# Scatters of an attention mask, issued by the state of a pacing clock instead of one per scan unit

## The chip, the cores and the metric

The kernel runs on one core of a Trainium2 chip. The metric is the device time of one execution in microseconds (us). The engines are called as in the profile: PE is TensorE, DVE is VectorE, ACT is ScalarE, POOL is GpSimd, SP is SyncE, which here only issues transfers.

## The reference

The input is four images of 32 x 32 positions with 256 channels, so 1024 tokens per image. Four layers follow each other:

- layer 0: layer norm, a projection to 512 channels, a 3 x 3 depthwise convolution, and a state space scan over the 1024 tokens with 64 states per channel, then a projection back and a residual;
- layer 1: a bottleneck with a grouped 3 x 3 convolution;
- layer 2: attention with 8 heads under a mask, then a mixture of 8 experts;
- layer 3: another state space scan with 16 states per channel, and a second mixture of experts.

The change concerns the mask of layer 2. It is built once from a list of edges and used for all four images:

```python
mask = jnp.zeros((N, N), dtype=bool).at[edge_index[0], edge_index[1]].set(True)
scores = jnp.where(mask[None, None], scores, -jnp.inf)
```

The scans are recurrences, for each channel d and state n:

```python
h = dA * h + (dtt * xt)[:, :, None] * Bt[:, None, :]
y = jnp.einsum('bdn,bn->bd', h, Ct)
```

## The kernel before, in words

**The scans.** The generator `scans` runs the recurrences as 1280 units in a fixed order of (layer, image), `SCANS`: image 0 of layer 0 first, units 0 to 255, four groups of 128 channels with 64 units each. A unit is 128 rows of 1024 steps. It loads `dA` with SP, takes its exponential on ACT, spreads the input over the rows with a matmul (`ps_rep`, two PSUM buffers), multiplies it by B on VectorE (`ps_rep<-ps_rep,rows`), runs the recurrence on VectorE (the SCAN instruction, `h<-dA,ps_rep`), and multiplies h by C on GpSimd (`h<-h,rows`, five buffers for h). Every two units TensorE collects h into `ps_y`, two units late. `scans` yields twice per unit.

**The side work.** Everything else is cut into `STAGES`, generators that yield after small pieces: four `front` stages (layer 0 up to its scan), `middle` (the rest of layer 0, layers 1 and 2, and layer 3 up to its scan) and `last`, one for each image. The first `front` also runs the preparation of weights (`prepare`). At its end each front makes the scan's inputs in eight items of 512 tokens (`steps`): ACT computes `sp_e` and `sp_l`, VectorE one operation on `sp_e`, GpSimd three on `sp_l` and `sp_r`, ACT and VectorE split the result into three bfloat16 `parts` (`sp_x` is the rest between them), GpSimd makes the last part, SP stores them. A stage that needs a scan's result waits (`Wait`) until that scan is issued: `middle` of image 0 needs all four groups of scan (0,0).

**The order.** Nothing is scheduled by hand on a time axis. The program wraps the engines in `Metered`, which adds an assumed cost of each instruction to a clock of its engine; `run` issues half a unit of a scan, and then pieces of side work until some clock is ahead of VectorE's. Every clock is held to at most 4 us (`LAG`) behind VectorE's. The assumed costs are the kernel's own: for GpSimd 2.3 ns a column for `tensor_tensor`, and 1.0 us for an indirect DMA.

**The mask.** The generator `mask_work` (`setup`, then `mask_prepare`, then `scatter`) sorts the edges' positions and then issues one indirect DMA after another on GpSimd, each of which writes 128 zeros into a DRAM tile that was filled with a large negative number (`mask_dram<-zero,where`). 64 are always issued. For 480 more there are four tests on GpSimd (`value_load` and `Switch`, lines 1134 and 1136) that jump over 32, 64, 128 and 256 of them when no row of edges has that many entries; with these inputs they are all jumped over. Then one DMA copies the mask to bfloat16 (`maskT<-mask_dram`, line 1142). The tile is read first by SP at line 1215, in the attention of image 0. `mask_work` is advanced in two places: in `need`, once for every piece of a stage that a scan has to wait for (this issues 22 scatters before unit 0), and in `run`, at every second yield of `scans`, that is behind each unit:

```python
for n, _ in enumerate(self.scans(mp, psum)):
    if n % 2:
        next(self.mask_work, None)
    now = clock["vector"]
```

So in the kernel before, the 42 scatters that are left stand one behind each of the units 0 to 41, the four tests behind units 43 to 46, and the copy behind the next.

Of the kernel before, what the change touches and what calls it, by code (L numbers as in the profile page):

```python
# [132 lines left out]
class Hybrid:  # L133
# [428 lines left out]
    def run(self):  # L562

        self.done, self.ready = set(), set()
        self.todo, self.stage, self.wait = list(STAGES), None, None
        self.alone = False
        nc, tc = self.nc, self.tc
        with tc.tile_pool(name="scan", bufs=1) as mp, tc.tile_pool(
            name="scps", bufs=1, space=PSUM
        ) as psum, tc.tile_pool(name="sdps", bufs=1, space=PSUM) as side, tc.manual_schedule():  # L570
            self.side_psum(side)
            self.mask_work, self.sorted = self.setup(), False
            clock = self.clock = dict.fromkeys(Metered.COST, 0.0)
            self.nc = Metered(nc, clock)
            for n, _ in enumerate(self.scans(mp, psum)):
                if n % 2:
                    next(self.mask_work, None)
                now = clock["vector"]
                for e in clock:
                    clock[e] = max(clock[e], now - LAG)  # L580
                for _ in range(TICKS):
                    if max(clock.values()) > clock["vector"] + LEAD or self.advance() is None:
                        break
            while self.advance() is not None:
                pass
            self.nc = nc
        assert not self.todo
# [588 lines left out]
    def attention(self, b, tb):  # L1176
        nc, tc, vec = self.nc, self.tc, self.vec
        with tc.tile_pool(name=f"at{b}", bufs=1, side="right") as op:
            xa = op.tile([P, TB, C], F32, name="xa")
            qT = op.tile([P, 2, L], F32, name="qT")  # L1180
            kT = op.tile([P, 2, L], F32, name="kT")
            v = op.tile([P, TB, C], F32, name="v")
            mT = op.tile([P, 2, L], BF16, name="mT")
            maskT = op.tile([P, TB, L], BF16, name="maskT")
            wo = self.weight(op, "L2_attn_Wo", 2)
            large = op.tile([1, 1], I32, name="large")
            nc.vector.memset(mT, 0.0)
            with tc.tile_pool(name=f"aa{b}", bufs=1, side="right") as fp:
                wq, wk, wv = (self.weight(fp, "L2_attn_" + n, 2) for n in ("Wq", "Wk", "Wv"))
                xT = fp.tile([P, 2, L], F32, name="xTa")  # L1190
                yield from self.norm(fp, tb, TB, xa, "lnt")
                yield from self.turned(xa, TB, xT)

                def project(item):
                    w, dst, bias, sc, c, g = item
                    ps = self.ps("ps_qk")
                    cols = slice(g * 512, (g + 1) * 512)
                    self.mm(ps, lambda k: w[:, k, c * P : (c + 1) * P], xT, 2, cols)
                    nc.scalar.activation(
                        dst[:, c, cols], ps, AF.Identity, bias=bias[:, c : c + 1], scale=sc  # L1200
                    )

                yield from self.pipe(
                    [
                        (w, dst, bias, sc, c, g)
                        for w, dst, bias, sc in (
                            (wq, qT, self.bq, self.isq), (wk, kT, vec["L2_attn_bk"], 1.0)
                        )
                        for c in range(2) for g in range(2)
                    ],  # L1210
                    project, cost=1.7,
                )

                yield from self.large_scores(fp, qT, kT, large)
                nc.sync.dma_start(maskT, self.mem[("maskT",)].rearrange("j p f -> p j f"))

                def values(j):
                    ps = self.ps("ps_v", (P, 2, C))
                    for i in range(2):
                        m = 2 * j + i  # L1220
                        for k in range(2):
                            nc.tensor.matmul(
                                ps[:, i, :], lhsT=xT[:, k, m * P : (m + 1) * P], rhs=wv[:, k, :],
                                start=(k == 0), stop=(k == 1),
                            )
                    nc.scalar.copy(v[:, 2 * j : 2 * j + 2, :], ps)

                yield from self.pipe(range(TB // 2), values, cost=1.7)
            go = nc.values_load(large, engines=self.sides, min_val=0, max_val=1)
            tc.mark_branch_hint_location(f"large{b}", go, engines=self.sides)  # L1230
            yield from self.add_rows(xa, self.bo, TB)
            yield from self.add_rows(tb, self.beta, TB)
            with tc.tile_pool(name=f"ab{b}", bufs=1, side="right") as fp:
                yield from self.shift(fp, qT, kT, mT, maskT, go, f"large{b}")
            with tc.tile_pool(name=f"ac{b}", bufs=1, side="right") as fp:
                yield from self.all_heads(fp, tb, qT, kT, v, maskT, mT, xa, wo)
# [694 lines left out]
```

## Time and profile before

| what | us |
|---|---|
| time, median of 3 runs (lowest to highest) | 6504.83 (6499.96 to 6507.34) |
| profiled execution, its own time | 6499.29 |
| its span in the profile | 6497.3 |
| VectorE busy | 5119.6 |
| TensorE busy | 5253.9 |
| GpSimd busy | 3646.8 |
| unit 0 of the scans starts (VectorE's timeline) | 152.6 |
| unit 258 starts | 1247.4 |

The span goes from the first to the last profiled instruction; the time of the execution is 2.0 us longer. A row of a timeline or of the groups reads: start and duration, engine, line, operation, written tile, read tiles, shapes, and in brackets the idle time of the engine before it with what ended it. A row of the table of stretches reads: the stretch, its length, busy time of each engine with its number of instructions, TensorE's granted clock, the share of the DMA engines' time, and GB/s. Nearly all instructions carry line 124, the helper that meters them, so they are told apart by tile.

### The profile page before, as it was taken

The page shows a single profiled execution, that of the slowest core. Times are in us where ns is not written, and L with a number is a line of the kernel's source. Part 1 is how long each engine was busy: PE and PEld are TensorE (multiplying, and loading weights), DVE is VectorE, ACT ScalarE, POOL GpSimd, SP SyncE. Part 2 cuts the span into 40 slices and gives each one's busy share as a digit, 9 for nine tenths or more (in the row PEclk, how much of TensorE's full clock was granted, in tenths as well). Part 3 has the DMA queues.
Part 4 walks back from the last instruction along what each step waited for, and adds up shares of the span by engine and source line. Part 5 has one row for each costly group of instructions (what it writes and reads, how often), then busy time and mean ns, then how long its engine had stood idle before and what let it go on. Part 6 is the DMA issues. An engine that isn't in the chain of part 4 may idle for free. (4 is left out here: it accounts for less than half of the span.)

```text
span 6497.3 us, 59722 instructions
## 1 busy us (share of the span) xinstructions
PE 5253.9 (81%) x20235; PEld 2124.1 (33%) x20320; DVE 5119.6 (79%) x4310; ACT 3415.4 (53%) x4095; POOL 3646.8 (56%) x1793
## 2 busy tenths in 40 slices
PE   6667868689797569979689679798699688978979
PEld 2022212222342022234145232252255222524656
DVE  3978988988898998889889988898899981258311
ACT  3346656355576335567568445577387354246311
POOL 2957677765557666555856665556756661055200
PEclk9577868689898569979789789898699689878989
DMA  2454554643355566335635664345544750156221
GB/s 101 145 163 159 180 163 160 198 150 124 119 174 170 180 169 164 113 128 184 195 132 176 195 159 135 112 146 178 182 164 163 196 148 15 46 147 166 68 67 34
DMA packets 348077, 936.58 MB, mean 144 GB/s; under 512 B 37140, under 2 KB 119648, under 8 KB 346144
## 3 DMA queue, kind: packets, MB, share of 16 engines
q1 hardware_dynamic: 345616, 930.35, 46.0%
q0 software_dynamic: 2128, 2.13, 0.2%
q8 instruction: 168, 2.75, 0.2%
q14 instruction: 165, 1.35, 0.1%
HBM read 842.59 MB, written 93.95 MB: 144 GB/s over the span
## 5 line engine op out<-in xcount | busy, mean ns | idle before, releaser
L124 POOL TENSOR_TENSOR h<-h,rows 128x1024 f32<-128x1024 f32 x1280 | 3033.0, 2372 | 1835.8 <-DVE h L124 1572.9
L124 DVE TENSOR_TENSOR_SCAN h<-dA,ps_rep 128x1024 f32<-128x1024 f32 x1280 | 2923.7, 2284 | 131.4 <-ACT dA L124 3.1
L124 DVE TENSOR_TENSOR ps_rep<-ps_rep,rows 128x1024 f32<-128x1024 f32 x1280 | 1551.7, 1212 | 188.5 <-PE ps_rep L124 183.9
L124 ACT ACTIVATE dA<-dA,A_L_conv_A_log 128x1024 f32<-128x1024 f32 x1024 | 1147.7, 1144 | 612.1 <-DMA dA<-dt 547.2
L124 PE MATMUL ps_rep<-S,spread_L_conv_A_log 96*128 96x512 bf16 x2048 | 763.2, 463 | 767.6 <-DVE h L124 716.2
L124 PE MATMUL ps_y<-h,collect_L_conv_A_log 128*32 128x512 f32 x4096 | 775.8, 767 | 61.5 <-POOL h L124 61.0
L124 PE MATMUL ps_h<-xTm,we 128*128 128x512 f32 x1536 | 714.2, 604 | 0.0
L124 PE MATMUL ps_e<-we,h_m 128*128 128x256 f32 x3072 | 700.4, 380 | 2.3 <-ACT h_m L124 2.3
L124 PEld LDWEIGHTS <-spread_L_conv_A_log 96*128 96x128 bf16 x2048 | 159.9, 103 | 1568.9 <-DVE h L124 1236.1
L124 ACT ACT_TABLE_LOAD x483 | 619.7, 1283 | 59.4 <-PE ps_h L124 44.1
L124 PEld LDWEIGHTS ps_e<-we,h_m 128*128 128x128 f32 x3072 | 579.4, 190 | 152.5 <-issue 61.1
L124 DVE SCALAR_TENSOR_TENSOR tb<-ps_e,cw,tb 128x256 f32<-128x256 f32 x512 | 219.9, 474 | 409.3 <-PE ps_e L124 409.2
L124 ACT ACTIVATE h_m<-ps_h,cols 128x512 f32<-128x512 f32 x384 | 260.2, 687 | 501.4 <-PE ps_h L124 498.9
L124 ACT ACTIVATE p<-ps_sc 128x512 f32<-128x512 f32 x432 | 234.5, 594 | 386.0 <-PE ps_sc L124 255.4
L124 PEld LDWEIGHTS ps_h<-xTm,we 128*128 128x128 f32 x1536 | 291.9, 193 | 331.7 <-issue 286.9
L124 ACT ACTIVATE dA<-dA,A_L_attn_A_log 128x1024 f32<-128x1024 f32 x256 | 290.6, 1146 | 200.0 <-DMA dA<-dt 172.3
L124 PE MATMUL ps_rep<-S,spread_L_attn_A_log 96*128 96x512 bf16 x512 | 185.8, 451 | 173.8 <-DVE h L124 161.0
L124 PE MATMUL ps_at<-p,v 128*32 128x512 f32 x1024 | 277.6, 623 | 4.8 <-ACT sums L124 4.6
L124 PE MATMUL ps_at<-p,ones 128*32 128x512 f32 x1024 | 277.6, 623 | 0.0
L124 PE MATMUL ps_sc<-qT,kT 32*128 32x512 f32 x864 | 262.9, 665 | 14.2 <-ACTq L1318 8.1
L124 PE MATMUL ps_cv<-pad,diag 128*128 128x512 f32 x576 | 262.3, 597 | 0.0
L124 PEld LDWEIGHTS ps_y<-h,collect_L_conv_A_log 128*32 128x32 f32 x4096 | 99.4, 119 | 436.9 <-issue 222.6
(327 smaller groups left out, 4865.4 us busy)
## 6 DMA issues: line engine op xcount, KB each, us to landing
dA<-dt SPq DMA_DIRECT2D x1280, 512.0 KB
we<-in_L_ffn_W_dram SPq DMA_DIRECT2D x64, 512.0 KB
parts<-parts SPq DMA_DIRECT2D x64, 384.0 KB
S<-parts SPq DMA_DIRECT2D x96, 256.0 KB
dt<-sp_r SPq DMA_DIRECT2D x64, 256.0 KB
y<-yo SPq DMA_DIRECT2D x128, 128.0 KB
y_back<-y SPq DMA_DIRECT2D x64, 256.0 KB
we<-in_L_ffn_w_dram SPq DMA_DIRECT2D x64, 256.0 KB
```

Of the source, the lines that this page charges most:

```text
L124: return got(*args, **kw)
```

## The change

There are two edits. In `run`, the mask's generator is advanced behind a unit only if GpSimd's pacing clock is behind VectorE's at that point; `now` is read one line earlier for that. In `attention`, whatever is left of the generator is issued before the mask is loaded.

```diff
@@ -573,9 +573,9 @@
             clock = self.clock = dict.fromkeys(Metered.COST, 0.0)
             self.nc = Metered(nc, clock)
             for n, _ in enumerate(self.scans(mp, psum)):
-                if n % 2:
+                now = clock["vector"]
+                if n % 2 and clock["gpsimd"] < now:
                     next(self.mask_work, None)
-                now = clock["vector"]
                 for e in clock:
                     clock[e] = max(clock[e], now - LAG)
                 for _ in range(TICKS):
@@ -1212,6 +1212,8 @@
                 )
 
                 yield from self.large_scores(fp, qT, kT, large)
+                for _ in self.mask_work:
+                    pass
                 nc.sync.dma_start(maskT, self.mem[("maskT",)].rearrange("j p f -> p j f"))
 
                 def values(j):
```

In the order of the built instructions this moves the scatters: those behind units 0 to 2 stay, the next 39 stand behind units 20 to 58, the four tests behind units 60 to 63, and the copy behind the next. Since a scatter also adds 1.0 us to GpSimd's pacing clock, the side work of the fronts is let through at other units too.

## The prediction

> **What bounds the kernel now.** I read, in this order, the busy shares of the page, the table of stretches, the waits and the timeline of GpSimd, and the timelines of VectorE and TensorE where VectorE stood still.
>
> ```profile
> span 6497.3 us, 59722 instructions
> PE 5253.9 (81%) x20235; PEld 2124.1 (33%) x20320; DVE 5119.6 (79%) x4310; ACT 3415.4 (53%) x4095; POOL 3646.8 (56%) x1793
> ```
>
> VectorE's 79% is an average: up to about 5300 us, where the scans run, it stands near 90%, and then a TensorE tail follows. I count scan units from 0 (the n-th SCAN row of VectorE's timeline). A unit with no side work takes 3.54 us (units 70 to 90 start 3.54 apart): a 1.21 us multiply and a 2.29 us scan. Every microsecond that VectorE loses in a unit is lost for good. These stretches are units 0 to 43, 43 to 55, 55 to 60, 60 to 93, 93 to 98, and five late items of front 3 (units 228 to 242):
>
> ```profile
> core 0: us, PE busy (x) PEld busy (x) DVE busy (x) ACT busy (x) POOL busy (x), PEclk, DMA share, GB/s
> 152.60:317.00 164.40, 111.97 (x255) 14.68 (x254) 151.47 (x91) 71.43 (x75) 150.23 (x92) 0.58 0.43 145
> 317.00:383.30 66.30, 35.62 (x77) 4.95 (x76) 48.46 (x31) 25.75 (x33) 47.87 (x29) 0.55 0.62 181
> 383.30:432.40 49.10, 23.77 (x62) 8.56 (x60) 30.32 (x58) 10.17 (x12) 18.20 (x10) 0.60 0.53 163
> 432.40:550.80 118.40, 114.36 (x388) 43.62 (x389) 112.83 (x67) 82.62 (x113) 76.69 (x33) 0.97 0.46 158
> 550.80:581.70 30.90, 23.20 (x71) 6.71 (x69) 19.05 (x13) 19.27 (x26) 16.77 (x9) 0.89 0.41 130
> 1121.60:1183.10 61.50, 42.29 (x100) 5.58 (x96) 60.88 (x41) 38.31 (x49) 60.72 (x36) 0.53 0.58 188
> ```
>
> In the first row, where the scatters are, GpSimd is as full as VectorE; in the fourth, where front 1 convolves, GpSimd is 65% busy. GpSimd's timeline shows why:
>
> ```profile
> 320.06 1.00 POOL L124 DMA_INDIRECT mask_dram<-zero,where  x1 [0.17 <-issue]
> 321.09 2.36 POOL L124 TENSOR_TENSOR h<-h,rows 128x1024 f32<-128x1024 f32 x1
> 330.26 2.35 POOL L124 TENSOR_TENSOR h<-h,rows 128x1024 f32<-128x1024 f32 x1 [6.82 <-issue]
> 336.98 1.15 POOL L124 TENSOR_TENSOR parts<-sp_x,parts 128x512 bf16<-128x512 f32 x1 [4.36 <-DVE ps_rep L124]
> 346.52 2.35 POOL L124 TENSOR_TENSOR h<-h,rows 128x1024 f32<-128x1024 f32 x1 [2.19 <-issue]
> ```
>
> A unit with a scatter costs GpSimd 2.37 + 0.17 + 1.00 = 3.54 us, VectorE's own pace, so nothing it does for front 0 (1.15 + 3 x 1.26 = 4.9 us an item) can be made up. The idle times of 6.82, 4.36, 2.19 and once more 4.36 us (before the multiply at 353.23) are the four tests on whether more scatters are needed, 17.7 us together. When GpSimd is late, TensorE's ps_y stands in front of the next ps_rep, and VectorE stops:
>
> ```profile
> 275.56 1.93 PE L124 MATMUL ps_y<-h,collect_L_conv_A_log 128*32 128x512 f32 x6 [7.50 <-POOL h L124]
> 278.50 1.23 DVE L124 TENSOR_TENSOR ps_rep<-ps_rep,rows 128x1024 f32<-128x1024 f32 x1 [5.02 <-PE ps_rep L124]
> 335.60 1.23 DVE L124 TENSOR_TENSOR ps_rep<-ps_rep,rows 128x1024 f32<-128x1024 f32 x1 [4.74 <-PE ps_rep L124]
> 342.71 2.16 DVE L124 TENSOR_TENSOR sp_x<-sp_l,parts 128x512 f32<-128x512 f32 x1 [5.88 <-ACT parts L124]
> ```
>
> [...] a scatter occupies 1.00 us, its landing takes 3.0 us (median of the 42 beside scans). [...]
>
> **The change part by part.** *Order.* The order of the built instructions, before against after, shows the counts and kinds unchanged. [...] All the side work of fronts 0 to 3 that followed unit 4 stands closer: from the preparation (units 55 to 60, now 21 to 26) on it is exactly 34 units earlier, with its own pattern kept. It ends near unit 220; then 38 bare units wait for scan (0,0). From unit 260 on the order is as before. Why: the pacing clock charged GpSimd 2.42 + 1.00 a unit against VectorE's 3.55, a credit of 0.13; without the scatter it is 1.13, and an item of front 0 is let through every third unit. The drain before the mask load costs nothing: the list is empty 224 units earlier. SP's 2,055 transfers move with their stages; none is added.
>
> *Sum, as excess over 3.54 us a unit.* Before: units 0 to 43, 164.4 - 152.2 = 12.2; 43 to 55, 66.3 - 42.5 = 23.8; 55 to 60, 49.1 - 17.7 = 31.4; 60 to 93, 118.4 - 116.8 = 1.6; 93 to 98, 30.9 - 17.7 = 13.2; 98 to 258, no different in the two kernels.
>
> After:
> - *Front 0's six items, units 0 to 21.* Same spacing as in the last row of the table: (61.5 - 15 x 3.54) / 5 = 1.7 us an item, 10 for six; 3 more since the first two stand two units apart. 13 in place of 36.0: **23 gained**. VectorE's own work for the items stays; the stalls go. Next late there is ACT's parts, 2 to 6 us late where items crowd (11.7 us in units 43 to 55); the 3 allows for one.
> - *Preparation, units 21 to 26.* 31.4 again. A unit lasts 9.8 us there, which covers a 3.5 us GpSimd turn; the mask copy (2 MB, landing 13.7 us) no longer precedes it, which could gain some microseconds, and a scatter caught in its loads could lose as many. Taken at 0, bounds -5 to +5.
> - *Scatters beside front 1, units 26 to 59.* GpSimd's turn of 3.54 to 3.55 us against 3.54 loses up to 0.01 x 34 = 0.3. What else stands behind a waiting scatter is the next h multiply, then ps_y. A scatter waits for its predecessor's landing; in units 0 to 43 that was 4.7 us in six waits, at a DMA share of 0.43, here 0.46. GpSimd can be about two units (7 us) late before TensorE notices, as few front operations need it there. **1 lost**, bounds 0 to 6; if the cover goes it is the 5.
> - *The tests, units 60 to 63.* The first two (11.2 us) fall in stalls that front 1 has there anyhow (VectorE waits 5.5 us for ps_rep, then 3.8 for sp_e). The last two and the late multiplies push front 1's first sp_l: recorded to end at 577.8, it would end near 559.1 + 6.8 + 2.4 + 4.4 + 2.4 + 2.2 + 2.4 + 4.4 + 3.8 = 587.9. VectorE's sp_x behind it comes 10 us later, and the items that follow keep GpSimd 98% busy, so nothing is won back. **10 lost**, bounds 0 [...] to 17.7. Before, the tests cost inside the 23.8.
> - *Bare units 220 to 258*: 3.54 us each, nothing to lose.
>
> Together 23 - 1 - 10 = **12 us gained**. After unit 260 the same instructions follow in the same order, so the gain is carried through VectorE's stretch to the tail. The profiled execution took 6499.3 us (span 6497.3), 5.5 under the median of 6504.8; its own sum is 6487.3, and at the median 6492.8, which I give as 6493.
>
> **The rivals.** *The tests are hidden whole* by front 1's stalls or run during the multiplies: 23 gained, 6482. For it: 9.3 us of stalls stand there; against it: 17.7 us do not fit, and in units 43 to 50 the tests did stop VectorE. *The loss is only moved*: the tests cost all 17.7 and scatters 5 in their new place, 23 - 23 = 0, 6505. For it: the same turns and tests meet a front that is dense on VectorE and ScalarE. *Scatters land late beside front 1*, and that ends slower. Each has 2.37 + 0.17 us of multiply to hide its landing in. If the mean wait for landing were 1.3 us, GpSimd's turn would be 4.85, and 39 scatters less 7 us of lateness allowed would lose 44: 23 - 10 - 44 = 31 slower, 6536. It decides from a mean wait of about 0.5 us ((12 + 1 + 7) / 39). Against it: the wait before was 4.7 / 42 = 0.11. For it: landings beside scans reached 5.7 us. *The change does nothing* can be ruled out, since the order of instructions differs.
>
> **How the numbers follow.** A measurement of this kernel can tell about 0.2%, 13 us. Main case 0.6, half of it over 13; hidden tests 0.17, all over; loss moved 0.14, nearly all within; late scatters 0.09, mostly slower. Faster 0.47, same 0.44, slower 0.09. The range goes from hidden tests with a lighter preparation, 6475, to the loss moved plus 5 us of preparation, 6510. The main case's own range is 6485 to 6502.
>
> **What would show it.** In the profile after: unit 21 starts near 152.6 + 21 x 3.54 + 13 = 240 (before 231), unit 55 near 152.6 + 55 x 3.54 + 13 + 31 + 3 = 394 (before 383.3), unit 64 near 152.6 + 64 x 3.54 + 13 + 31.4 + 2.6 + 23.2 = 449, unit 258 near 1235 (before 1247.4). GpSimd's waits for mask_dram beside front 1 under 8 us would confirm the scatter term; VectorE's idle time at units 60 to 66 is the tests' term. Units 0 to 21 with more than 25 us of excess, or a time that returns after unit 258, would make me wrong.

## The result, and the profile after

The changed kernel takes 6487.2 us (median of 18 runs, 6478.1 to 6496.4) against 6504.6 us (18 runs, 6493.0 to 6515.2): a ratio of 0.9973, 95% interval 0.9965 to 0.9980, that is 17 us less, between 13 and 23. The forecast was 12 less.

The head of the page of the changed kernel:

```profile
span 6481.8 us, 59799 instructions
PE 5240.9 (81%) x20320; PEld 2121.8 (33%) x20320; DVE 5121.5 (79%) x4310; ACT 3415.5 (53%) x4095; POOL 3649.2 (56%) x1793
```

Busy times are as before (TensorE's 5241 us against 5254, the others within 3 us); what changed is idle time. The table of stretches of the changed kernel, cut at its units 0, 21, 26, 59 and 64, and from 64 to 220 and 220 to 258:

```profile
core 0: us, PE busy (x) PEld busy (x) DVE busy (x) ACT busy (x) POOL busy (x), PEclk, DMA share, GB/s
156.50:241.90 85.40, 54.52 (x130) 7.82 (x132) 84.06 (x55) 57.17 (x71) 81.57 (x48) 0.52 0.55 173
241.90:290.80 48.90, 24.56 (x62) 9.71 (x60) 30.29 (x59) 10.38 (x13) 21.98 (x14) 0.53 0.52 161
290.80:413.90 123.10, 117.19 (x388) 44.26 (x389) 112.90 (x66) 82.34 (x113) 106.96 (x63) 0.96 0.49 158
413.90:458.00 44.10, 25.76 (x71) 6.88 (x69) 20.64 (x13) 19.34 (x26) 21.41 (x13) 0.72 0.38 116
458.00:1102.50 644.50, 468.49 (x1426) 127.47 (x1426) 596.29 (x403) 395.98 (x514) 496.70 (x257) 0.71 0.56 178
1102.50:1237.50 135.00, 74.75 (x228) 8.84 (x228) 129.60 (x77) 43.82 (x41) 89.53 (x39) 0.50 0.52 164
```

In the first row VectorE is busy 84.1 of 85.4 us while front 0 finishes. In the third GpSimd is now 107 us busy of 123, against 77 of 118 in the same work before: the scatters have moved here. The fourth, with the tests, lasts 44.1 us against 30.9 of the same front work before. The fifth is the same work as the kernel before did in this row of its own table:

```profile
581.70:1233.20 651.50, 472.26 (x1426) 128.44 (x1426) 596.72 (x404) 396.21 (x514) 497.14 (x257) 0.71 0.54 177
```

As excess over 3.54 us a unit, which is how the prediction counts:

| work | before | forecast | after |
|---|---|---|---|
| front 0's rest (after: units 0 to 21; before: 0 to 55, with scatters and tests) | 36.0 | 13 | 11.1 |
| preparation (21 to 26; before 55 to 60) | 31.4 | 31.4 | 31.2 |
| front 1's convolution (26 to 59; before 60 to 93) | 1.5 | 2.6 | 6.3 |
| start of front 1's items (59 to 64; before 93 to 98) | 13.2 | 23.2 | 26.4 |
| the rest of the fronts (64 to 220; before 98 to 254) | 99.3 | 99.3 | 92.2 |
| bare units (220 to 258; before 254 to 258) | 0.0 | 0 | 0.5 |
| sum (of the unrounded values) | 181.5 | 169.5 | 167.7 |

So units 0 to 258 took 1081.0 us instead of 1094.8. Unit 0 started 3.9 us later in this execution, and units 258 to 1279 took 4804.3 us instead of 4810.7. Both are differences between executions: over the twelve profiles, runs of both kernels and of all variants below that load 12 units ahead, the start lies anywhere from 151.4 to 156.8 us, the later stretch from 4800 to 4814, and neither goes with the order of instructions.

GpSimd's timeline of the changed kernel where the tests stand, and VectorE behind it:

```profile
420.50 1.00 POOL L124 DMA_INDIRECT mask_dram<-zero,where  x1 [3.03 <-DMA mask_dram<-zero,where]
428.22 2.38 POOL L124 TENSOR_TENSOR h<-h,rows 128x1024 f32<-128x1024 f32 x1 [4.33 <-issue]
436.07 2.35 POOL L124 TENSOR_TENSOR h<-h,rows 128x1024 f32<-128x1024 f32 x1 [5.47 <-issue]
442.89 2.34 POOL L124 TENSOR_TENSOR h<-h,rows 128x1024 f32<-128x1024 f32 x1 [4.48 <-PE ps_dt L124]
449.47 1.26 POOL L124 TENSOR_TENSOR sp_l<-sp_l,sp_e 128x512 f32<-128x512 f32 x1 [4.24 <-issue]
454.10 2.16 DVE L124 TENSOR_TENSOR sp_x<-sp_l,parts 128x512 f32<-128x512 f32 x1 [13.65 <-ACT parts L124]
```

The rows are a late scatter, then three multiplies and front 1's first sp_l, each behind one of the four tests. (By GpSimd's own multiplies the tests stand behind units 59 to 62, and behind 42 to 45 in the kernel before, one unit earlier than counted above.) VectorE's sp_x stands in front of all that VectorE has to do next, and waits 13.65 us. So GpSimd's late turn is still there, in one place.

### The profile page after: what moved, and what is told of

Its sections match the earlier page's. It is cut to its first block, busy times and chain, and to the rows that moved or that the text cites. A ratio compares the mean times of both kernels' runs of the same rounds, so it can differ in the third digit from the quotient of the medians.

```text
span 6481.8 us, 59799 instructions
## 1 busy us (share of the span) xinstructions
PE 5240.9 (81%) x20320; PEld 2121.8 (33%) x20320; DVE 5121.5 (79%) x4310; ACT 3415.5 (53%) x4095; POOL 3649.2 (56%) x1793
## 5 line engine op out<-in xcount | busy, mean ns | idle before, releaser
L124 PE MATMUL ps_y<-h,collect_L_conv_A_log 128*32 128x512 f32 x4096 | 744.1, 767 | 15.6 <-POOL h L124 15.6
L124 POOL TENSOR_TENSOR sp_l<-sp_l,sp_e 128x512 f32<-128x512 f32 x62 | 78.5, 1266 | 276.5 <-DVE sp_e L124 252.3
```

The lines of the kernel that those rows point to most:

```text
L124: return got(*args, **kw)
```

## The experiments

The theory: GpSimd was full where the scatters stood (busy 150 of 164 us in units 0 to 43), and the tests made it later (17.7 us of idle time); in the new place both cost less but not nothing. All ratios are against runs of the kernel before on the same chip.

**Both kernels once more.** No edit.

> The changed kernel once more, unaltered. Theory (a full GpSimd and the four tests explain the gain, all of it before unit 64): 0.9973 of before again; units 0 to 64 last within 1 us of the first profile of the changed kernel (156.5 to 458.0), while the 7 us that units 64 to 220 and the 6 us that units 258 to 1279 took less than in the profile of before are differences between executions and come out otherwise. Rival (the earlier side work also speeds up what follows): both come out again within 2 us.

> The kernel before once more, unaltered, for a second profile. Both theories: within 0.2% of before. Theory: units 0 to 64 take what they took (152.6 to 448.0, within 1 us or so), units 98 to 254 may differ from the 651.5 us of the first profile by as much as the changed kernel's 644.5 did.

The changed kernel came to 0.9970 of before (0.9960 to 0.9980), the kernel before to 0.9997 (0.9988 to 1.0005). Of the changed kernel units 0 to 21 took 85.4 us again, 26 to 64 took 167.6 after 167.2. In the kernel before units 0 to 55 took 233.7 us after 230.7, so that a difference of 3 us in one profile tells nothing there. But the 7 us of units 64 to 220 also came again: 646.3 after 644.5, against 653.4 after 651.5 in the kernel before. This part of the theory fell; the experiment on SP's loads below finds its cause. The 6 us after unit 258 did not come again (4813.1 us there, 4808.8 in the kernel before).

**The tests taken out of each kernel.** The generator still yields at these points, so nothing else moves. With these inputs no scatter that is left out would be issued.

```diff
-            go = nc.gpsimd.value_load(self.more[:, i : i + 1], min_val=0, max_val=1)
-            clock = dict(self.clock)
-            for arm in tc.Switch({mybir.EngineType.Pool: go}, 2):
...
-            self.clock.update(clock)
             yield
```

> The kernel before with the four tests on GpSimd and the 480 scatters that they jump over left out, everything else in its place. Theory: the stalls of VectorE at units 46 (10.6 us beyond its own work) and 49 (5.2) are GpSimd's time in the tests; without them 11 to 16 us less, about 0.998 of before. Rival (front 0's chain from ScalarE over VectorE to GpSimd is slow by itself when its items crowd): 0 to 3 us less.

> The changed kernel with the four tests and the 480 scatters behind them left out, everything else in its place. Theory: VectorE's 13.7 us wait for parts at unit 63 is the tests; 11 to 14 us less than the changed kernel, about 0.9954 of before. Rival (that wait is front 1's own latency, as in the kernel before at unit 97): 0 to 2 us less, 0.997 of before.

Kernel before: 0.9981 (0.9972 to 0.9990), 12 us; units 43 to 55 fell from 66.3 us to 53.6. Changed kernel: 0.9947 (0.9933 to 0.9960), 6472.8 us against 6484.2 of the changed kernel on the same chip; units 59 to 64 fell from 43 and 44 us to 31.6. VectorE's row there, without the tests:

```profile
436.64 1.68 DVE L124 TENSOR_TENSOR sp_x<-sp_l,parts 128x512 f32<-128x512 f32 x1 [1.68 <-ACT parts L124]
```

13.65 us of waiting became 1.68. The tests cost about 12 us in either place: the change gained nothing on them that can be told from the noise.

**The scatters taken out of each kernel.** Only those beside the scans; the clock is charged for them. The same edit sets the mask's fill, `NEG`, to -10.

```diff
                 for j in range(first, end):
-                    zeros(j)
+                    if j < 22:                    # 25 in the changed kernel
+                        zeros(j)
+                    else:
+                        self.clock["gpsimd"] += 1.0
                     yield
```

> The kernel before without the 42 scatters beside the scans; the pacing clock is charged for them as before, so the rest keeps its order, and the four tests stay. The mask therefore lacks those zeros, and its fill is -10 so that all sums stay finite. Theory: GpSimd is no longer full in units 0 to 43, their excess over 3.54 us a unit falls from 12.2 to 5 (three items of front 0); units 43 to 55 stay: 7 us less, 0.9989 of before. Rival (the scatters fit in GpSimd's turn and cost nothing): 0 us. If it reached 17 us, the order of the side work would have no part in the gain.

> The changed kernel without the 39 scatters from unit 20 on; the pacing clock is charged for them as before. The mask lacks those zeros, and its fill is -10. Theory: the one stall beside front 1, 4.8 us at unit 54, came from a scatter that waited 3.8 us for the landing of its predecessor; it goes, and preparation keeps its time: 5 us less than the changed kernel. Rival (that stall is TensorE's convolution): 0 us less.

Kernel before: 0.9981 (0.9975 to 0.9988), 12 us where 7 were expected. The expected part is there, and a second beside it (units 0 to 43 and 43 to 55, to be read against 164.40 and 66.30 us):

```profile
152.30:309.50 157.20, 89.47 (x258) 11.43 (x260) 152.03 (x91) 71.14 (x75) 112.55 (x53) 0.50 0.48 152
309.50:370.50 61.00, 33.49 (x80) 4.61 (x76) 50.25 (x32) 25.44 (x32) 45.21 (x28) 0.53 0.72 201
```

7.2 us less beside the scatters, and 5.3 less beside the tests, where no scatter stands: GpSimd no longer arrives there late. In front of the tests it began the multiply of unit 42 5.3 us after the scan's end in the kernel before, and 0.14 us without scatters. The first test is shorter too, an idle time of 3.2 us instead of 6.8: with the scatters in, GpSimd stands at this test until 325.75 us, and the last scatter, issued at 320.06, had landed at 325.73. Scatters and tests are not two separate costs, since lateness is handed on and the first test waits for the last scatter. In the changed kernel the same holds: units 26 to 59 fell from 123.1 to 118.2 us and units 59 to 64, with the tests in place, from 44.1 to 36.8, together 12 us where 5 were expected; the time came to 0.9958 (0.9943 to 0.9973). The changed kernel's stall at unit 54, 4.8 us, had this cause and is gone. It had come behind this scatter of the changed kernel:

```profile
389.14 1.00 POOL L124 DMA_INDIRECT mask_dram<-zero,where  x1 [3.79 <-DMA mask_dram<-zero,where]
```

**The side work early, the scatters where they were.**

```diff
-            "indirect_dma_start": lambda **_: 1.0,
+            "indirect_dma_start": lambda **_: 0.0,
```

> The kernel before with nothing charged to GpSimd's pacing clock for a scatter. The scatters stay behind units 0 to 41, but the side work comes even earlier than in the changed kernel (front 0 is done at unit 17 or 18, all fronts 37 units earlier). Theory (where the scatters stand counts): GpSimd has 3.54 us a unit and 4.9 us an item of front 0 in every three units, 15.5 us against VectorE's 12.4, so six items lose 19 us less 7 of lateness allowed, 12 more than in the changed kernel; the tests fall beside the convolution of front 1 and cost some 6 less: about 11 us under before, 0.9983. Rival (the earlier side work alone makes the gain): 17 us or more under before, 0.9973 or less.

1.0006 (0.9998 to 1.0014), where the theory had 0.9983 and its rival 0.9973: nothing gained at all. Units 0 to 18 and 18 to 23, front 0's rest and the preparation:

```profile
152.90:244.40 91.50, 48.93 (x107) 7.07 (x108) 75.45 (x49) 54.92 (x69) 81.31 (x54) 0.56 0.45 144
244.40:299.30 54.90, 25.63 (x70) 9.91 (x64) 30.40 (x59) 9.51 (x13) 28.44 (x19) 0.56 0.47 147
```

An excess of 27.8 and 37.2 us, against 11.1 and 31.2 in the changed kernel. With a scatter in every unit, VectorE waits 14.8 us for parts in the first stretch, where the changed kernel's waits for 0.3. So the rival is out for this order: the side work brought forward gained nothing while the scatters stayed in its way. The theory's direction held, its size did not: 17 us lost at the items instead of 12, 6 more in the preparation, and scatters and tests were hardly cheaper beside the convolution (units 23 to 61 have 30.6 us of excess, units 26 to 64 of the changed kernel 32.7). How much of the 17 us is the scatters' is open, because front 0's rest is also packed into 18 units here instead of 21. The version with room for both, below, packs it into 19 with a single scatter among them, and has 17.9 us of excess there and 5.4 us of waits for parts. The order of the changed kernel with the scatters left at units 0 to 41 was not run.

**The tests moved to the bare units.**

```diff
+            while self.unit < 216 + 8 * i:        # self.unit is n // 2 in run
+                yield
             go = nc.gpsimd.value_load(self.more[:, i : i + 1], min_val=0, max_val=1)
```

> The changed kernel with the four tests moved into the bare units, behind units 223, 231, 239 and 247, eight units apart; the copy of the mask follows. Theory: a test of 2 to 7 us makes GpSimd late by no more than TensorE's queue allows, and eight bare units with 1.16 us to spare make it up, so the tests cost 0 to 3 us there: 10 to 13 us less than the changed kernel, about 0.9956 of before. Rival (a test costs its time wherever it stands, as each engine jumps with it): within 3 us of the changed kernel, 0.997 of before.

0.9948 (0.9934 to 0.9961), 6473.1 us: all that taking the tests out gave, with the tests in. Units 220 to 258 took this long with them, and two of the four tests look like this in GpSimd's timeline:

```profile
1092.10:1226.80 134.70, 75.44 (x228) 9.49 (x228) 129.65 (x77) 43.83 (x41) 89.88 (x40) 0.53 0.58 180
1115.05 6.97 POOL L124 TENSOR_TENSOR h<-h,rows 128x1024 f32<-128x1024 f32 x3 [3.97 <-issue]
1143.02 7.02 POOL L124 TENSOR_TENSOR h<-h,rows 128x1024 f32<-128x1024 f32 x3 [3.59 <-issue]
```

38 x 3.54 is 134.5. Behind each test GpSimd runs two or three multiplies without a gap, has caught up, and no wait of VectorE is recorded in these units.

**Neither scatters nor tests in the changed kernel.** Both edits together.

> The changed kernel without the 39 scatters from unit 20 on and without the four tests (the pacing clock is charged for the scatters as before; the mask lacks those zeros, its fill is -10). Theory: what is left of the mask's cost beside the scans goes, units 26 to 59 at 1.4 us of excess, units 59 to 64 at 13.2 as in front 1 of the kernel before: 6 + 12 = 18 us less than the changed kernel, about 6468. Rival (scatters and tests each cost their own 10 and 17 us as timed): 27 us less, about 6459.

0.9945 (0.9932 to 0.9958), 6465.7 us. Units 26 to 64 took 151.1 us, against 167.2: 16 less, near the theory's 18 and not the 27 of two separate costs.

**A version with room for both.** The tests as above, and a scatter only behind every second unit, where the clock is over 1 us behind.

```diff
-                if n % 2 and clock["gpsimd"] < now:
+                if n % 4 == 3 and clock["gpsimd"] < now - 1.0:
```

> All scatters and tests are issued, but spread: a scatter only behind every second unit and only where GpSimd's pacing clock is over 1 us behind (units 21 to 63 and 85 to 121), the tests eight units apart in the bare units (226 to 250). Theory: GpSimd has 1.16 us to spare in a bare unit and so 2.3 in two, a scatter takes 1.2; it comes to the kernel without scatters and tests within 5 us, about 6470. Rival (scatters and tests cost wherever they stand): as the changed kernel, 6485.

0.9953 (0.9940 to 0.9966), 6472.7 us, 7 us above the kernel without scatters and tests where at most 5 were expected, with intervals that overlap. Units 24 to 57 and 57 to 62 (the same work as 26 to 64) took 149.9 us with 19 of the scatters in them, against 158.6 with only the tests spread. This beats both kernels, but not the version with only the tests spread (0.9948): that version's front 0 has 11.1 us of excess and this one's, packed into 19 units, 17.9, so that units 0 to 258 took 1068.6 us here and 1070.0 there. What the scatters gained beside front 1 was for the most part lost in front 0.

**Where the 7 us come from.** In the kernel before, units 247 and 250 lose 1.7 and 4.6 us over 3.54; SP's queue and VectorE there:

```profile
1192.81 1.18 SPq L401 DMA_DIRECT2D rows<-bc  x2
1194.03 1.54 SPq L408 DMA_DIRECT2D S<-parts  x3
1196.18 1.24 SPq L830 DMA_DIRECT2D y_back<-y  x2
1210.58 1.72 SPq L830 DMA_DIRECT2D y_back<-y  x2
1205.89 2.29 DVE L124 TENSOR_TENSOR_SCAN h<-dA,ps_rep 128x1024 f32<-128x1024 f32 x1 [1.85 <-ACT dA L124]
1219.67 1.28 DVE L124 SCALAR_TENSOR_TENSOR y_back<-u_back,cols,y_back 128x1024 f32<-128x1024 f32 x1 [3.26 <-DMA y_back<-y]
```

The inputs of scan (0,1), two loads of 512 KB and three of 256 KB, go out just before middle 0 loads its first y_back; the load at 1210.58 is its third. The changed kernel starts middle 0 34 units earlier, where no scan begins. So in the kernel before:

```diff
-AHEAD = 12
+AHEAD = 16
```

> The kernel before with a scan's inputs loaded 16 units ahead in place of 12, so that the loads of rows and S for scan (0,1), 1.8 MB, stand behind unit 239 and not just in front of the first y_back of middle 0. Theory (in the kernel before y_back waits behind these loads, in the changed one middle 0 starts 34 units earlier and meets none): units 98 to 254 take 645 to 648 us in place of 651.5 to 655. Rival (the 7 us come from something else in the 34 units): 651 us or more again. The time changes by 5 us or so, which other loads may hide.

Units 98 to 254 took 646.3 us, and VectorE's y_back row has lost its wait:

```profile
1221.04 1.26 DVE L124 SCALAR_TENSOR_TENSOR y_back<-u_back,cols,y_back 128x1024 f32<-128x1024 f32 x1
```

Not all of the 7 us is at these two units, some is spread over fronts 2 and 3, but the loads carry most of it. The time came to 0.9966 (0.9953 to 0.9979), 22 us by this ratio, where 5 or so were expected. In the profile most of it lies later: units 258 to 1279 took 4791.7 us, below the 4800 to 4814 of all profiles with 12. That loads and waits meet there in the same way is not shown. Units 43 to 60 took 120.2 us against 115.4 and 116.5 in the two profiles of the kernel before, so the earlier loads may also cost something.

**Both together.**

> The spread scatters and tests together with scan inputs loaded 16 units ahead. Theory: the two act in different places; the 5 us at units 247 to 250 are in the spread version already, the rest of what the earlier loads gave (17 us after unit 258) comes on top: 17 less than the spread version, about 6455. Rival (both fill the same idle time): as the spread version, 6472.

0.9938 (0.9924 to 0.9951), 6463.4 us; units 258 to 1279 took 4793.8 us. This is the lowest time of the versions that keep the whole mask, some 23 us under the changed kernel by the ratios. At the medians it is 9 us under the version with room for both, in the profile of units 258 to 1279 16; the theory had 17 and its rival 0, and since the two intervals overlap the times alone decide for neither.

## Why the prediction was right

The direction, the main mechanism and the range held; 12 us were forecast, 17 came. That the size came so near is in part luck: the terms that the prediction named come to 7 us in the first pair of profiles and 9 in the second, and 7 more came from a term that it put at nothing. Step by step:

- **Front 0 without scatters.** Forecast 13 us of excess in place of 36.0, measured 11.0 to 11.1 in each of the six profiles with this order. The two removals in the kernel before, 12 us each, show where the loss came from, and with the side work early and the scatters left there nothing was gained. What the closer order alone gives or costs was not separated.
- **Preparation.** Forecast unchanged, measured 31.2 and 30.7. The cover held: one scatter waited 5.1 us there for a predecessor that landed after 8.2 us, and the excess did not grow. The mask copy's absence bought nothing.
- **Scatters beside front 1.** Mis-sized: 1 us forecast, 5 measured (6.3 less 1.5; 4.9 us went when they were taken out). In four profiles with these scatters in place the excess was 6.3, 7.7, 5.5 and 10.1, a loss of 4 to 9 us. One wait of 3.8 us came through as a stall of 4.8, and the sign given for the step (under 8 us of waits) was just met with 7.3 in units 26 to 59, with 3.0 more in front of the tests. The step that failed is the 7 us of lateness that were allowed. TensorE is busy 117 of 123 us in these units, which leaves it little to catch up with; that this is the reason is argued, not shown.
- **The tests.** 10 us forecast, 13 and 12 measured in the two profiles. The mechanism was the one named, and the first two did fall into front 1's stalls, which lasted 5.5 and 3.8 us as in the kernel before. The prediction added the terms; the runs showed that about 7 us of the tests' loss depended on the scatters. It also took the idle time of 6.82 us for the first test alone, where 2.3 us of it are a wait for the last scatter to land.
- **Units 98 to 258 no different.** This step failed, by 7 us in the right direction. The prediction noted that SP's transfers move with their stages, and did not ask what else is in SP's queue at the old and at the new place. The scan's own loads stand at fixed units, and moving middle 0 by 34 took it out of their way.
- **Bare units.** Forecast nothing, measured 0.5.
- **After unit 260.** Forecast carried through. No loss in that stretch goes with the order.

Together 25 - 5 - 13 + 7 = 14 us in the first profiles, and 16 in the second pair (1098.9 less 1082.7); the interval of the times, 13 to 23, does not tell these from the 17 of the medians.

Of the rivals, the wholly hidden tests are out: they cost 12. The loss that is only moved was right for the scatters (5 in their new place) and for the tests in kind (12 before, 12 after), but it had the tests at 17.7 and so no gain. Late landing was real but too small: 15.4 us of waits in 39 scatters, the 5.1 in the preparation among them, is 0.39 a scatter, where the break-even was 0.5 and the rival had 1.3.

## What to carry to other kernels

Look for the stretch in which a helper engine's turn is as long as that of the engine that bounds, here 3.54 us against 3.54: nothing there can be made up, and lateness is handed on to the next thing the helper does, here 5.3 us of it to the tests. Put such work where the helper's turn is shorter, as in the bare units (2.36 us against 3.54), and in pieces with room behind each; here four tests cost 12 us in a row and nothing eight units apart. When a block of work is moved, compare both ends of the move with what stands at fixed places in the queues, as the loads of a scan's inputs do here, which carried most of 7 us. And when delays share an engine, do not add their prices: here 12 us for the scatters and 12 for the tests of the changed kernel were 16 together.

## What the runs showed of the hardware that was not expected

The same test on GpSimd, a loaded value and a jump over instructions, left it idle for 6.8, 4.4, 2.2 and 4.4 us in the kernel before, and for 4.0, 3.6, 3.4 and 3.6 us in the bare units; the distance jumped (32 to 256 scatters) does not order these times. The records of waits and branches in GpSimd's trace show part of what they consist of. In the kernel before, the first test waits 4.2 us for the landing of the last scatter, of which 2.3 lie behind the end of the multiply in front. Each test then has one record of a semaphore operation, 1.44 to 1.47 us long in both kernels, and from the branch behind it to the next record 2.8, 2.5, 2.5 and 2.7 us pass in the kernel before, 2.6, 3.8, 2.5 and 2.6 in the changed kernel. Part of this, too, runs beside a multiply: at the third test of the kernel before, the 1.45 us begin at 342.41, in a multiply that lasts from 341.99 to 344.33. Where the tests are, the profile also has packets of 8 KB on a DMA queue of kind "instruction" (q14): twelve stand between 321 and 357 us of the kernel before, where its tests are, none in the 31 us ahead of them; twelve between 423 and 450 us of the changed kernel, where its tests are, and one in its stretch from 321 to 357. What GpSimd does in the 2.5 us behind the branch, and whether these packets have to do with it, is not shown.

VectorE lost time at the same units each time: unit 161 of the kernel before lasted 7.1 us in each of five profiles, the corresponding unit 127 with the other order 4.9 us in each of six, while the whole time varies by 20 us between executions.
